# Attention and a gated feed-forward on one core: weight transfers in SyncE's queue, and another grouping in the last tile

## The chip, the core and the metric

The kernel runs on one core of a Trainium2 chip. A core has a matrix engine (TensorE, PE in the profile, with its weight loads apart as PEld), three engines for elementwise work (VectorE or DVE, ScalarE or ACT, GpSimd or POOL) and SyncE (SP), which computes nothing and issues transfers. Each engine works through its own instruction list in order and waits at semaphores for the others. A transfer (DMA) is issued by an instruction of SP, ACT or POOL, and then 16 DMA engines carry it out. The metric is the time of one execution on the device in microseconds (us).

## The reference

One block of a network on `x` of shape (4, 1024, 256): 16 heads of attention with 16 features each, then a feed-forward part with weights of -1, 0 and 1.

```python
def attention(x, Wqkv, Wout):
    q, k, v = split_heads(x @ Wqkv.T)                    # 16 heads of 16
    scores = q @ k.T / 4
    e = exp(clip(scores - max(scores), -50, 50))
    return join_heads(e / (e.sum() + 1e-6) @ v) @ Wout.T

def feed_forward(x):
    h = silu(x @ w1.T * w1_s) * (x @ w2.T * w2_s)        # 256 -> 1024
    h = gelu(h @ h1.T * h1_s)                            # 1024 -> 1024
    h = gelu(h @ h2.T * h2_s)
    return h @ w3.T * w3_s                               # 1024 -> 256

x = x + layernorm(attention(layernorm(x)))
x = x + layernorm(feed_forward(layernorm(x)))
```

## The kernel before

**Stages.** After a prologue of some 40 us, attention runs to about 640 us, and the feed-forward part from there to the end. Attention goes over 4 batches `b`, 4 groups `g` of 4 heads, 2 halves `h` of 512 queries, and 8 blocks of 128 keys; a *unit* is one (b, g, h). For each pair of heads and block of keys, TensorE makes scores (L470, tile `s`), ScalarE their exponentials (L471, tile `e`, in a ring of 8), and TensorE weighs the values with them (L478, tile `acc`). At a unit's end VectorE copies the accumulator out (`o<-acc`, L270).

**The order.** It is written out by hand. The loop at the end of `tile_fast` alternates between making exponentials and weighing, and calls `side.take()` once in a turn of about three tiles of exponentials. `Side` holds chains of `Step`s; a step is taken when the number of turns in its `gap` has passed since the chain's last step, and its flag `tensor` says whether it needs TensorE. What a step issues goes into the lists of its engines at that place. The chains that matter here:

- `stack` (L432): 32 copies of 64 KB (L418) from the projections `cq`/`ck` into the tiles `sq` and `sk`, from which the scores of the next group but one are made. All are issued by SP. There are two sets of these tiles, so that a set has to land before its group begins.
- `divide` (L500): at a unit's end SP stores `top`, the running largest exponentials, to DRAM (`top_d<-top`, L505), and two turns later (`back`, L508) loads them in another layout (`folded<-top_d`). VectorE reduces them (`fold`, L512), TensorE transposes the accumulator (`po`, L517), and VectorE divides. In SP's list both transfers stand between the stack copies.
- `load_rest` (L195): the remaining inputs, by SP, one in a turn: rows of `x` for later batches, `wo_sb`, scales.
- `round_weights` (L243): rounds the weights of the feed-forward part once, in 22 blocks of 512 KB: `load` to the tile `w` (one buffer), `cast` to `wr` (one buffer[...]) on GpSimd, and a store to the DRAM tile `rounded`. Load and store are issued by GpSimd, the store in the step that casts. `load_weights` (L745, SP) reads `rounded` from 567 us on.

GpSimd has few other tasks in this stage: putting values into slots (`vaug`, L448), the powers in the norms (`rstd`, L105), and small squares (`sum`, L350).

**The feed-forward part** goes over 8 tiles of 512 tokens. In each, `gated` makes the first product, `gelu_layer` twice the next two (L802), and `finish` (L842) the last: 4 runs of 128 tokens, each 16 matmuls (L855: 8 blocks of weights, with a high and a low half). In seven tiles the norm and the residual that follow are spread over the next tile by `side`. In the last tile `finish` does them itself, for two runs at a time: product with `w3s_sb` (L857), statistics (L95, L96), `ve` (L103), the power on GpSimd (L105), scaling (L113), residual (L863), and one store a run (L867).

A flag in `bad`, counted along the way, says whether the fast path was valid; the program ends with a branch on it (L67, L68).

Of the kernel before, what the change touches and what calls it, by code (L numbers as in the profile page):

```python
# [9 lines left out]
F32 = mybir.dt.float32  # L10
# [28 lines left out]
TPQ = NQ // P  # L39
# [77 lines left out]
def tile_fast(ctx: ExitStack, tc: tile.TileContext, x, wqk, wv, wo, w1, w1s, w2, w2s, h1, h1s, h2, h2s, w3, w3s, out, bad):  # L117
    nc = tc.nc
# [20 lines left out]
    def pieces(h, view):  # L139

        t, n = NH + (TPQ - 1) * h, TPQ * h
        return (slice(n, n + 1), view[:, h : h + 1, :]), (slice(n + 1, n + TPQ), view[:, t : t + TPQ - 1, :])
# [19 lines left out]
    weights = {"w1": w1, "w2": w2, "w3": w3, "h1": h1, "h2": h2}  # L162
    rows_at_once = {n: WIDE // w.shape[1] for n, w in weights.items()}
# [4 lines left out]
    rounded = {n: dram.tile(list(w.shape), F32R, name=f"{n}_r") for n, w in weights.items()}  # L168
# [11 lines left out]
    with ExitStack() as actx, ExitStack() as rctx:  # L180
# [62 lines left out]
        def round_weights(n, c):  # L243

            st = {}

            def rows(w):
                return w[c * P : (c + rows_at_once[n]) * P, :].rearrange("(i p) d -> p i d", p=P)

            def load():  # L250
                st["w"] = work.tile([P, WIDE], F32, tag="w", name="w", bufs=1)
                nc.gpsimd.dma_start(out=st["w"].rearrange("p (i d) -> p i d", i=rows_at_once[n]), in_=rows(weights[n]))

            def cast():
                st["r"] = work.tile([P, WIDE], F32R, tag="wr", name="wr", bufs=1)
                nc.gpsimd.tensor_copy(st["r"], st["w"])
                nc.gpsimd.dma_start(out=rows(rounded[n]).bitcast(F32), in_=st["r"].bitcast(F32).rearrange("p (i d) -> p i d", i=rows_at_once[n]))

            return [Step(load, 1, False), Step(cast, 3, False)]

        def by_slots(o, w, i, **flags):

# [474 lines left out]
        halves_of = [(b, h) for b in range(B) for h in range(NH)]  # L737
# [18 lines left out]
        def norm_steps(tiles, st):  # L756


            def gather(i):
                def run():  # L760
                    st["mv"] = norms.gather(tiles()[i : i + 2], i, st.get("mv"))

                return run

            def root():
                st["ln"] = norms.root(st["mv"])

            return [Step(gather(i), 1, False) for i in range(0, TPQ, 2)] + [Step(root, 0, False)]
# [73 lines left out]
        def finish(n, i):  # L842

            b, h = halves_of[n]
            st = {}
            z = both.tile([P, TPQ, D], F32, tag="y", name=f"z_{n}", bufs=1)

            pairs = [ps.tile([P, 2, NQ], F32, tag="big", name="pz") for _ in range(TPQ // 2)]
            p = [pairs[t // 2][:, t % 2, :D] for t in range(TPQ)]
            for t0 in range(0, TPQ, 2):  # L850
                ts = range(t0, t0 + 2)
                for c in range(HC):
                    for t in ts:
                        for k, half in enumerate(i):
                            nc.tensor.matmul(p[t], half[:, c, t * P : (t + 1) * P], homes["w3"][c], start=c == 0 and k == 0, stop=c == HC - 1 and k == 1)  # L855
                for t in ts:
                    nc.vector.tensor_mul(z[:, t, :], p[t], w3s_sb)  # L857
                if n == len(halves_of) - 1:

                    ln = norms.stats([z[:, t, :] for t in ts])  # L860
                    for j, t in enumerate(ts):
                        norms.apply(z[:, t, :], z[:, t, :], ln, j)
                        nc.vector.tensor_add(z[:, t, :], z[:, t, :], xs[b][:, h * TPQ + t, :])  # L863
                        for at, tokens in pieces(h, out[b].rearrange("(t p) d -> p t d", p=P)):
                            k = h * TPQ + t - at.start
                            if 0 <= k < at.stop - at.start:
                                nc.sync.dma_start(out=tokens[:, k, :], in_=z[:, t, :])  # L867
            if n == len(halves_of) - 1:
                return []

            def apply(i0):
                def run():
                    for t in range(i0, i0 + 2):
                        norms.apply(z[:, t, :], z[:, t, :], st["ln"], t)

                return run

            def add(t):
                def run():
                    nc.vector.tensor_add(z[:, t : t + 2, :], z[:, t : t + 2, :], xs[b][:, h * TPQ + t : h * TPQ + t + 2, :])  # L880

                return run

            def store():
                for at, tokens in pieces(h, out[b].rearrange("(t p) d -> p t d", p=P)):
                    nc.sync.dma_start(out=tokens, in_=z[:, at.start - h * TPQ : at.stop - h * TPQ, :])

            return (
                norm_steps(lambda: [z[:, t, :] for t in range(TPQ)], st)
                + [Step(apply(i), 1, False) for i in range(0, TPQ, 2)] + [Step(add(t), 1, False) for t in range(0, TPQ, 2)] + [Step(store, 0, False)]  # L890
            )
# [41 lines left out]
        def feed_forward():  # L933

            chain = ends[B - 1, NH - 1]
            checks = check_weights()
            for n in range(len(halves_of)):

                gated(ffn["a"], 2 if n else 1)
                if n + 1 < len(halves_of):  # L940
                    chain[0].extend(prepare(n + 1, to_scalar))

                if 1 < n < len(halves_of) - 1:
                    size = -(-len(checks) // (len(halves_of) - 3))
                    side.add(sum(checks[size * (n - 2) : size * (n - 1)], []) + (judge() if n == len(halves_of) - 2 else []))
                gelu_layer(ffn["b"], ffn["a"], "h1")
                gelu_layer(ffn["a"], ffn["b"], "h2")
                side.flush()
                chain = side.add(finish(n, ffn["a"]), True)
            side.flush()  # L950
# [36 lines left out]
        begin(0)  # L987
        side.add(stack(0, 1) + few(load_rest(), 1))
        side.add([s for k in blocks for s in round_weights(*k)])
        made = seen = weighed = 0  # L990

# [7 lines left out]
        while weighed < len(tiles):  # L999
            n = end = made  # L1000
# [3 lines left out]
            if made == len(tiles):  # L1004
                n = made
# [4 lines left out]
            if n - weighed >= 4 and made - weighed + TURN - 2 <= RING and tiles[weighed][3] != NT - 2 and side.next_is_heavy():  # L1010
                n = weighed + 2
# [257 lines left out]
```

## Time and profile before

| | |
|---|---|
| median of 3 runs | 1302.34 us (1301.2 to 1303.02) |
| profiled execution, its own time | 1304.9 us |
| its span, first to last instruction | 1303.1 us |
| mean granted TensorE clock | 0.990 |
| loads of a block of weights by POOL (L252) | 22: 6 with a median of 6.1 us to landing, 16 with 6.4 |
| stores of a block by POOL (L257) | 22: 4.6 and 4.0 us |
| casts of a block on POOL (L256) | 22 of 1.04 us (median), from 43 to 394 us |
| last instruction of VectorE | ends at 1295.05 us |

How to read the views of the profile: a group of instructions is named by its line and engine and the tiles that it writes and reads (`out<-in`). "Idle before" is the time that the engine stood still just before, with what ended it after an arrow. The chain that ended last is followed back from the last instruction, at each step to what released it. Engines with a q (SPq) are queues of instructions that issue or wait. A window view has one line for a stretch of time: its length, then busy time and number of instructions of PE, PEld, DVE, ACT and POOL, the granted TensorE clock, the busy share of the DMA engines, and GB/s. In the DMA view, a line of an issue ends with the median time from issue to landing; q1 (hardware_dynamic) is the queue of SP, q0 (software_dynamic) that of POOL.

### The profile page before, as it was taken

The numbers are of one execution on the slowest core, as the hardware profiler recorded it, in microseconds if no ns is written. First come the engines' busy times: TensorE is split into PE (matmuls) and PEld (weight loads), VectorE is DVE, ScalarE is ACT, GpSimd is POOL, SyncE is SP. The second block draws the span as 40 slices with busy tenths as digits, with TensorE's granted clock in tenths as the row PEclk, the third lists the DMA queues.
The fourth block names the chain that finished last, engine by engine and source line by source line (L and its number), as shares of the span: only waits on it lengthen the run. The fifth ranks groups of instructions, "written<-read, shape, count | busy, mean of one in ns | idle before, by whom it ended". The sixth has DMA issues, their size and how long they took to land.

```text
span 1303.1 us, 21108 instructions
## 1 busy us (share of the span) xinstructions
PE 1246.2 (96%) x8104; PEld 771.5 (59%) x8104; DVE 700.2 (54%) x1578; ACT 721.6 (55%) x902; POOL 119.4 (9%) x166
## 2 busy tenths in 40 slices
PE   7998899999989999989999999999999999999995
PEld 2333333333333333323688888888888888888885
DVE  3465447763577545656653634636446464463533
ACT  3897898899888998998521413314233142231410
POOL 6221012211111000000000000000000000000000
PEclk8998999999999999999999999999999999999998
DMA  4775745666553544453230000201102011020000
GB/s 131 205 185 137 190 116 144 163 174 153 137 125 77 98 83 98 92 129 120 82 146 1 25 1 1 65 25 34 56 1 66 25 33 57 1 65 9 17 1 20
DMA packets 65678, 107.02 MB, mean 82 GB/s; under 512 B 12960, under 2 KB 39200, under 8 KB 65568
## 3 DMA queue, kind: packets, MB, share of 16 engines
q1 hardware_dynamic: 57680, 80.93, 25.4%
q0 software_dynamic: 7360, 24.12, 6.0%
q8 instruction: 66, 1.08, 0.3%
q10 hardware_dynamic: 528, 0.52, 0.2%
q14 instruction: 44, 0.36, 0.1%
HBM read 48.38 MB, written 23.59 MB: 55 GB/s over the span
## 4 chain that ended last, share of the span: by engine, by line
PE 74%; ACT 10%; DVE 8%; issue 3%; DMA 2%; POOL 1%; SPq 1%; ACTq 0%; POOLq 0%; DVEq 0%
PE ph L802 36%; PE acc L478 12%; ACT e L471 8%; PE s L470 8%; PE pz L855 4%; PE pg L802 4%; PE p L264 4%; PE py L264 2%; PE pv L264 2%; DVE sg L818 2%; PE po L517 1%; DVE ha_lo L807 1%; DVE top L487 1%; DVE st L95 1%; ACT sg L816 1%
## 5 line engine op out<-in xcount | busy, mean ns | idle before, releaser
L471 ACT ACTIVATE e<-s 128x1024 f32<-128x1024 f32 x512 | 483.8, 1043 | 43.6 <-PE s L470 36.2
L478 PE MATMUL acc<-e,vaug 128*32 128x512 f32 x2048 | 257.3, 605 | 1.0 <-POOL vaug L448 1.0
L838 ACT ACTIVATE a<-ph,h_scale 128x512 f32<-128x512 f32 x128 | 81.0, 685 | 301.4 <-PE ph L802 301.4
L470 PE MATMUL s<-sq,sk 64*128 64x512 f32 x1024 | 189.5, 447 | 22.2 <-ACT e L471 17.2
L802 PE MATMUL ph<-hb_hi,h 128*128 128x512 f32 x512 | 199.6, 390 | 0.0
L802 PE MATMUL ph<-hb_lo,h 128*128 128x512 f32 x512 | 199.4, 390 | 0.0
L470 PEld LDWEIGHTS s<-sq,sk 64*128 64x128 f32 x1024 | 87.3, 186 | 144.0 <-ACT e L471 116.5
L487 DVE TENSOR_TENSOR top<-top,e 128x512 f32<-128x512 f32 x192 | 134.0, 698 | 31.7 <-ACT e L471 26.5
L105 POOL TENSOR_TENSOR rstd<-ve,minus_half 128x4 f32<-128x4 f32 (+1 forms) x33 | 37.0, 1122 | 826.2 <-DVE ve L103 826.2
L478 PEld LDWEIGHTS acc<-e,vaug 128*32 128x32 f32 x2048 | 49.4, 109 | 106.5 <-issue 100.2
L802 PEld LDWEIGHTS ph<-hb_hi,h 128*128 128x128 f32 x512 | 96.1, 188 | 20.2
L802 PEld LDWEIGHTS ph<-hb_lo,h 128*128 128x128 f32 x512 | 96.2, 188 | 20.0
L839 DVE CAST ha_hi<-a 128x512 fp32r<-128x512 f32 x64 | 27.1, 423 | 142.7 <-ACT a L838 142.7
L802 PE MATMUL ph<-ha_hi,sq 128*128 128x512 f32 x256 | 101.9, 398 | 0.4
L802 PE MATMUL ph<-ha_lo,sq 128*128 128x512 f32 x256 | 99.9, 390 | 0.0
L802 PE MATMUL ph<-ha_lo,sk 128*128 128x512 f32 x256 | 99.8, 390 | 0.0
L802 PE MATMUL ph<-ha_hi,sk 128*128 128x512 f32 x256 | 99.8, 390 | 0.0
L816 ACT ACTIVATE sg<-pg,w_scale 128x512 f32<-128x512 f32 x64 | 43.3, 688 | 56.0 <-DVE ha_lo L807 45.6
L818 DVE SCALAR_TENSOR_TENSOR sg<-pg,w_scale,sg 128x512 f32<-128x512 f32 x64 | 47.1, 745 | 46.3 <-ACT sg L816 46.1
L839 DVE CAST hb_hi<-a 128x512 fp32r<-128x512 f32 x64 | 27.0, 422 | 71.5 <-ACT a L838 71.5
L264 PE MATMUL p<-xT,wqk_sb 128*32 128x512 f32 x512 | 61.3, 600 | 3.7 <-DVE on L495 1.4
L802 PEld LDWEIGHTS ph<-ha_hi,sq 128*128 128x128 f32 x256 | 48.1, 188 | 13.1 <-DVE sg L818 3.4
(164 smaller groups left out, 1637.3 us busy)
## 6 DMA issues: line engine op xcount, KB each, us to landing
w<-in_h_dram POOLq DMA_DIRECT2D x16, 512.0 KB, 6.4
h_r<-wr POOLq DMA_DIRECT2D x16, 512.0 KB, 4.0
x<-in_h_dram SPq DMA_DIRECT2D x32, 256.0 KB, 2.6
top_d<-top SPq DMA_DIRECT2D x30, 256.0 KB, 2.3
folded<-top_d SPq DMA_DIRECT2D x30, 256.0 KB, 3.2
sk<-ck1hi SPq DMA_DIRECT2D x64, 64.0 KB, 2.7
sk<-ck1lo SPq DMA_DIRECT2D x64, 64.0 KB, 2.7
sq<-cq1hi SPq DMA_DIRECT2D x64, 64.0 KB, 2.5
```

Of the source, the lines that this page charges most:

```text
L105: nc.gpsimd.tensor_tensor(rstd[:, :n], ve[:, :n], self.minus_half[:, :n], ALU.pow)
L264: nc.tensor.matmul(o[j : j + SLOT, :], w[:, j : j + SLOT], i, **flags)
L470: nc.tensor.matmul(s[:, a, :], stacks[1, g % 2, u][r, c * P : (c + 1) * P], stacks[0, g % 2, u][r, h * NQ : (h + 1) * NQ], start=True, sto ...
L471: nc.scalar.activation(pair(k)[:, u], s, AF.Exp)
L478: nc.tensor.matmul(acc[SLOT * i : SLOT * (i + 1), :], vaug[g % 2][:, c, i, :], pair(k)[:, i // 2, i % 2, :], start=c == 0, stop=c == NT - 1)
L487: nc.vector.tensor_max(top, top if c > 1 else pair(k - 2)[:, :, :, 0:P], pair(k)[:, :, :, 0:P])
L802: nc.tensor.matmul(p, homes[n][c][:, m * P : (m + 1) * P], half[:, c, :], start=c == 0 and k == 0, stop=c == len(homes[n]) - 1 and k == 1)
L816: nc.scalar.activation(sg, p[:, 0, :], AF.Silu, scale=scales["w1"][:, m : m + 1])
L818: nc.vector.scalar_tensor_tensor(sg, p[:, 1, :], scales["w2"][:, m : m + 1], sg, ALU.mult, ALU.mult)
L838: nc.scalar.activation(a, p[:, j, :], AF.Gelu, scale=scales[n][:, m : m + 1])
L839: nc.vector.tensor_copy(o[0][:, m, :], a)
L855: nc.tensor.matmul(p[t], half[:, c, t * P : (t + 1) * P], homes["w3"][c], start=c == 0 and k == 0, stop=c == HC - 1 and k == 1)
```

## The change

In `round_weights`, load and store are issued by SP instead of GpSimd. The store is taken out of the step `cast` and becomes a step of its own, two turns later. In `finish`, for the last tile alone, the runs of tokens are grouped as (0, 1), (2), (3) instead of (0, 1), (2, 3): the matmuls of run 2 are all issued ahead of those of run 3, and each of the two has its own statistics, power and scaling.

```diff
             def load():
                 st["w"] = work.tile([P, WIDE], F32, tag="w", name="w", bufs=1)
-                nc.gpsimd.dma_start(out=st["w"].rearrange("p (i d) -> p i d", i=rows_at_once[n]), in_=rows(weights[n]))
+                nc.sync.dma_start(out=st["w"].rearrange("p (i d) -> p i d", i=rows_at_once[n]), in_=rows(weights[n]))
 
             def cast():
                 st["r"] = work.tile([P, WIDE], F32R, tag="wr", name="wr", bufs=1)
                 nc.gpsimd.tensor_copy(st["r"], st["w"])
-                nc.gpsimd.dma_start(out=rows(rounded[n]).bitcast(F32), in_=st["r"].bitcast(F32).rearrange("p (i d) -> p i d", i=rows_at_once[n]))
-
-            return [Step(load, 1, False), Step(cast, 3, False)]
+
+            def store():
+                nc.sync.dma_start(out=rows(rounded[n]).bitcast(F32), in_=st["r"].bitcast(F32).rearrange("p (i d) -> p i d", i=rows_at_once[n]))
+
+            return [Step(load, 1, False), Step(cast, 3, False), Step(store, 2, False)]
...
-            for t0 in range(0, TPQ, 2):
-                ts = range(t0, t0 + 2)
+
+            for ts in [(0, 1), (2,), (3,)] if n == len(halves_of) - 1 else [(0, 1), (2, 3)]:
                 for c in range(HC):
                     for t in ts:
                         for k, half in enumerate(i):
```

The changed kernel is two lines longer from the store on, so that L418, L470 and L855 of before are L420, L472 and L857 of after.

## Prediction

> **What bounds the kernel now.** I read the engines and the whole chain first, then the windows by unit of attention, then the chain in the odd units, then the DMA queues, then the end.
>
> ```profile
> PE 1246.2 (96%) x8104; PEld 771.5 (59%) x8104; DVE 700.2 (54%) x1578; ACT 721.6 (55%) x902; POOL 119.4 (9%) x166
> ...
> PE 74%; ACT 10%; DVE 8%; issue 3%; DMA 2%; POOL 1%; SPq 1%; ACTq 0%; POOLq 0%; DVEq 0%
> ```
>
> TensorE bounds the span; POOL, whose queue is relieved, is 9% busy and 1% of the chain. DMA and SP's queue hold 3% of the chain, some 39 us, and the chain of waits puts all of it before 165 us. So the edited transfers can pay only there. The windows, cut where accumulators are copied out, show it unit by unit (length, then busy time of PE, PEld, DVE, ACT, POOL, granted clock):
>
> ```profile
> 87.50:112.10 24.60, 20.62 (x142) 7.25 (x141) 11.03 (x23) 17.92 (x22) 1.81 (x2) 0.86 0.45 104
> 112.10:129.60 17.50, 16.87 (x133) 6.32 (x137) 11.31 (x20) 16.06 (x20) 5.42 (x8) 1.00 0.84 194
> 129.60:151.90 22.30, 18.92 (x148) 6.62 (x141) 8.83 (x21) 17.21 (x21) 0.93 (x2) 0.92 0.74 189
> ```
>
> The first and third are longer than the second by 7.1 and 4.8 us, and the clock fell in them. The timeline tells the first:
>
> ```profile
> 97.83 0.53 SPq L505 DMA_DIRECT2D top_d<-top  x1
> ...
> 100.46 0.36 SPq L508 DMA_DIRECT2D folded<-top_d  x1
> ...
> 103.24 0.75 DVE L512 TENSOR_TENSOR folded<-folded 128x256 f32<-128x256 f32 x2 [5.37 <-DMA folded<-top_d]
> ...
> 104.82 1.12 PE L517 MATMUL po<-ident,o 128*128 128x128 f32 x4 [3.57 <-DVE cq0lo L330]
> ```
>
> VectorE waits 5.37 us for `folded`, and TensorE 3.57 us behind VectorE. Its unit ended at 87.5, but SP reached the store of `top` at 97.83: from 70.72 on SP issued 37 DMAs without pause. At 0.62 us each, the pace of L418, that is 22.9 us, not 27.1: 4.2 us are lengthened issues and gaps. From 111.35 to 147.3 SP issues 48 DMAs, again late, with 5.7 us of such excess, and at 146.89 TensorE had waited 1.93 us for the last `sq` copy. Both stalls are followed by the half clock: 0.50 in 103.43:110.26 and in 147.81:151.22.
>
> What lengthens SP's issues is the other queue. Shares of the engines in 193:196, just after a store and a load by POOL at 191.3 and 191.8, then landing times of `folded` in 64:165 (POOL's transfers present) and in 402:560 (none):
>
> ```profile
> q0 software_dynamic: 199, 0.75, 93.2%
> q1 hardware_dynamic: 25, 0.04, 3.3%
> ...
> folded<-top_d SPq DMA_DIRECT2D x5, 256.0 KB, 4.4
> ...
> folded<-top_d SPq DMA_DIRECT2D x9, 256.0 KB, 3.2
> ```
>
> SP's queue moves almost nothing while POOL's has data, so `folded` takes 4.4 instead of 3.2 us (8.1 at worst), and `sk<-ck1lo` 4.8 instead of 2.3.
>
> **What the Trainium skill says.** "DMA: Bandwidth & Descriptors", Queues, rings and completion order: each of the 16 engines goes round its queue rows and drains a whole packet before it switches. The 93.2% against 3.3% agree as to direction, and are more one-sided than turn by turn. The same page, Issuing engines are not separate DMA queues: starting DMAs from several engines saves only the time to initiate them; by that the move costs SP 44 issues and little else, and the 3.2 to 4.4 us show that the choice of queue matters here beyond it. "TensorE: Matmul & The Clock Gate", Part 1: a free-running window of some 3.4 us with too little work halves the clock. The trace agrees: TensorE was busy 1.25 us in 100:103.43 and 1.22 in 144.4:147.81, and each was followed by 0.50.
>
> **Part 1, the transfers.** Removed: 44 POOL issues (22 loads, 22 stores) at 0.53 to 0.60 us, some 25 us of POOL; worth nothing, as POOL waits 826 us for `ve` alone. Added: 44 SP issues at 0.62 us (an estimate from the 64 KB copies), 27 us. SP's queue waits 89.5 us, 15 times, for the last `top` of a unit in 33:395; those waits hide the issues outside 70.7 to 98 and 111 to 147. The built program's order leaves TensorE, ScalarE and VectorE as they were up to the last tile. A block's steps take 6 turns instead of 4, so the last store moves from 395 to about 535 us; the first reader (L745) issues at 567.7: 32 us to spare. On POOL only the casts move, later.
>
> New waits: the cast waits for a load in SP's queue, and the store (SP) for the cast. Behind the store stand SP's stack copies and `back`, for which TensorE and VectorE wait. I put each block into the trace's times: load issued after its SP neighbour, landed 4.7 us later, cast 1.2 us, not before its POOL neighbour. Of the 22 casts the tightest ends 4.7 us before SP gets to its store, and none ends after its next POOL instruction is due. So no new stall; price 0, and without that cover up to 5 us each.
>
> In the two stretches where SP is late:
> - 70.72 to 97.83: one store (before the copy at 83.21) and one load (at 87.97) come in: 2 x 0.62 = 1.2. Their own bulk: in the reload of h2 512 KB pass every 1.3 us (landings 656.28, 657.95, 659.21), of which I take half as felt by SP, 0.7 each: 1.4 (bounds 0 and 2.6). The 4.2 of excess falls to the 0 to 1.2 seen in stretches after 402, say 0.6, to which the 1.4 is added. Net -4.2 + 0.6 + 1.4 + 1.2 = -1.0; bounds -2.4 and, if nothing of the excess was POOL's, +3.8. The wait of 2.27 us for `folded` at 82.3 also shrinks, but the end of this stretch is SP's, so I count nothing.
> - 111.35 to 147.3: one store (123.68) and one load (135.11), again 1.2 + 1.4. Of 5.7 excess some 2.5 is the x loads' own (they land after 4.3 to 4.9 us). Net -5.7 + 2.5 + 2.6 = -0.6; bounds -3.1 and +3.8. With landing quicker too (4.5 to 2.3 us for a late copy), I take 1.5 of the 1.93 us off.
> - The clock: 6.83 and 3.41 us at half cost 3.4 and 1.7 us of TensorE's work. With its gap cut to some 0.4 us the second goes, 1.7; the first gap (3.57 less 1.0) stays wide, 0 taken, 3.4 possible.
> - Small VectorE waits for `folded` at 200 and 259 (0.97, 0.37): they go, 0.3 taken.
>
> Sum: -1.0 - 1.5 - 1.7 - 0.3 = **-4.5**.
>
> **Part 2, the last tile.** The 64 matmuls stay; runs 2 and 3 are no longer interleaved. The timeline of the end:
>
> ```profile
> 1290.48 0.75 DVE L857 TENSOR_TENSOR z<-pz,w3s_sb 128x256 f32<-128x256 f32 x2
> ...
> 1292.65 0.69 POOL L105 TENSOR_TENSOR rstd<-ve,minus_half 128x2 f32<-128x2 f32 x1 [3.78 <-DVE ve L103]
> 1293.39 0.41 DVE L113 TENSOR_SCALAR z<-z,mv,rstd 128x256 f32<-128x256 f32 x1 [0.88 <-POOL rstd L105]
> ```
>
> TensorE is done at about 1289.8; VectorE is busy with runs 0 and 1 until 1290.56. So run 2 comes earlier from TensorE (about 1287.9) and nobody can take it: VectorE's order is written out. Its own chain sets the end. Before: 1290.56 to 1295.05, 4.49. Now, for each run: product 0.33, statistics 0.35 + 0.18, `ve` 0.18, POOL's round trip 0.84, scale 0.42, sum 0.43, four steps of 0.02: 2.8; twice 5.6. One more `ve` and one more trip, that were shared. **+1.1** (bounds 0.9 and 1.3). The last store's 1.7 us and the 6 us to the end of the program remain behind it.
>
> **Sum.** -4.5 + 1.1 = -3.4 against the profiled execution's 1304.9 (span 1303.1, 1.8 around it), so 1301.5; it stood 2.6 above the median 1302.34 of runs from 1301.2 to 1303.02, so 1298.9, said as **1299**. About 0.2% (2.6 us) is what a measurement of this kernel can tell from no change; the forecast lies just beyond it.
>
> **Rivals.**
> - *Hidden: no difference.* SP loses the excess but pays it back with the issues, 0 to -1.5; the tail's 1.1 stands; 1301.9 to 1303.4. For it: net -1.0 and -0.6 above are small differences of larger numbers. Against: the landing times of 402:560.
> - *SP's ring fills: slower.* One mechanism: in the two late stretches each 512 KB stands in the same ring ahead of copies, and they land after it. Excess unchanged, 4 x (0.62 + 1.3) = 7.7, less what slack of the copies takes (about 2), plus 1.1: 1305 to 1309; with another half-clock window of 1.7 to 3.4, up to 1312. It decides once what the four cost exceeds the share of the 9.9 us excess that POOL made. Against it: SP's x loads, 1 MB together, already pass there.
> - *Both stalls vanish: much faster.* 3.57 + 3.4 + 1.93 + 1.7 = 10.6, less 1.1: 1292.8. For it: when the gap at 104.82 falls below about 2 us, the clock would stay up too.
> - *The tail does what it seems to be for*, an earlier finish: only if VectorE waited for TensorE at 1290.56; it did not. It cannot be over 0.8, TensorE's lead; 3 in 100, inside the others.
>
> **How the numbers follow.** Forecast (1295 to 1299.7) 0.40 and much faster 0.12: faster 0.52. Hidden, with what small losses and gains balance: 0.31. Slower 0.17. The range 1292.5 to 1308 takes in the much faster case and the ring's lower end, and leaves out about 2 in 10; the forecast's own range is 1295 to 1301.
>
> **What would show it.** Right: no software queue after 34 us; `folded` near 3.2 us in 64:165; the unit that ends near 112 still over 20 us, the next but one near 19; no half clock near 148; 5.6 us from the third product to the last sum. Wrong: SP waiting at the store for POOL, a cast holding `rstd` or `vaug`, copies landing over 4 us after issue between 400 and 535, or TensorE gaps over 1 us where a group begins.

## The result, and the profile after

The changed kernel took 1295.67 us (median of 5 runs, 1295.29 to 1297.94) where the kernel before took 1302.97 (5 runs, 1301.2 to 1303.48). The ratio is 0.995, with a 95% interval of 0.9936 to 0.9965: faster by 0.5%. The profiled execution of after took 1295.67 us (span 1293.9).

The profiled execution of before took 1304.9 us, 1.9 above its median, and so the two spans differ by 9.2 us where the medians differ by 7.3. Cut at the last copy of an accumulator in attention, at the first `pz` of the last tile and at VectorE's last instruction, the 9.2 us lie so (the last column is what the prediction's sum gives):

| stretch | before | after | difference | predicted |
|---|---|---|---|---|
| to the end of attention | 628.82 | 619.91 | -8.9 | -4.5 |
| from there to the last tile's first `pz` | 653.13 | 652.98 | -0.2 | 0 |
| last tile, first `pz` to VectorE's end | 13.09 | 15.39 | +2.3 | +1.1 |
| VectorE's end to the end of the program | 8.01 | 5.60 | -2.4 | 0 |

Three terms of the sum were wrong, by 4.4, 1.2 and 2.4 us, and the second error, in the tail, offsets part of the other two.

**Attention.** The windows of after, by unit as in the prediction (length, busy time of PE, PEld, DVE, ACT and POOL, clock, DMA share, GB/s):

```profile
87.40:107.70 20.30, 18.71 (x142) 6.31 (x141) 10.86 (x23) 18.08 (x22) 1.04 (x1) 1.00 0.59 151
107.70:124.40 16.70, 16.34 (x129) 6.21 (x133) 10.75 (x20) 15.27 (x19) 2.15 (x3) 1.00 0.67 154
124.40:143.20 18.80, 17.62 (x151) 6.38 (x144) 9.41 (x20) 17.66 (x21) 1.05 (x1) 1.00 0.66 157
```

From copy to copy the three units took 24.6, 17.5 and 22.2 us before and take 20.3, 16.7 and 18.8 now, 8.5 less in all, with no half clock in any of them. The other units together are as long as before within 0.4 us. The timeline of the first of them shows why:

```profile
94.89 0.53 SPq L507 DMA_DIRECT2D top_d<-top  x1
...
97.53 0.35 SPq L510 DMA_DIRECT2D folded<-top_d  x1
...
100.32 0.75 DVE L514 TENSOR_TENSOR folded<-folded 128x256 f32<-128x256 f32 x2 [2.54 <-DMA folded<-top_d]
...
101.92 0.66 PE L519 MATMUL po<-ident,o 128*128 128x128 f32 x4 [0.76 <-DVE cq0lo L332]
```

SP reaches the store of `top` at 94.89 instead of 97.83. All that follows comes 2.9 us earlier, and TensorE's gap shrinks from 3.57 to 0.76 us. What made SP late is visible in SP's own timeline. First before, from about 74 us, where two of the pairs of copies take 2.2 to 2.4 us to issue (GpSimd has just issued a store and a load of a block), then after, where the same two pairs take 1.2, as most pairs do in both:

```profile
73.04 0.54 POOL L257 DMA_DIRECT2D w_r<-wr  x1 [0.30 <-POOL wr L256]
73.58 0.60 POOL L252 DMA_DIRECT2D w<-in_w_dram  x1
...
74.22 2.23 SPq L418 DMA_DIRECT2D sk<-ck1hi  x2
...
78.86 2.42 SPq L418 DMA_DIRECT2D sk<-ck1hi  x2
```

```profile
74.12 1.21 SPq L420 DMA_DIRECT2D sk<-ck1hi  x2
...
77.67 1.23 SPq L420 DMA_DIRECT2D sk<-ck1hi  x2
...
80.89 0.37 SPq L259 DMA_DIRECT2D w_r<-wr  x1
...
85.72 0.41 SPq L252 DMA_DIRECT2D w<-in_w_dram  x1
```

The block's own store and load are issued in 0.37 and 0.41 us, less than a 64 KB copy. The DMA view of after in 64:165 (queues with packets, MB and share; then issues, with the median time to landing) has no software queue any more:

```profile
q1 hardware_dynamic: 13088, 16.28, 66.0%
...
folded<-top_d SPq DMA_DIRECT2D x6, 256.0 KB, 2.9
...
sk<-ck1lo SPq DMA_DIRECT2D x16, 64.0 KB, 2.3
```

`folded` landed after 4.4 us here before, `sk<-ck1lo` after 4.8. The second is the safer sign: in kernel 2 below, whose attention is that of before, the two medians are 3.2 and 4.4.

**The last tile.** The timeline of its end in after:

```profile
1281.41 0.42 DVE L859 TENSOR_TENSOR z<-pz,w3s_sb 128x256 f32<-128x256 f32 x1
...
1281.88 0.58 PE L857 MATMUL pz<-ck1hi,ha_hi 128*128 128x256 f32 x1 [3.09 <-DVE z L859]
...
1285.06 0.28 PE L857 MATMUL pz<-ck1lo,ha_lo 128*128 128x256 f32 x1
1285.38 0.42 DVE L859 TENSOR_TENSOR z<-pz,w3s_sb 128x256 f32<-128x256 f32 x1 [1.09 <-PE pz L857]
...
1287.85 0.42 DVE L865 TENSOR_TENSOR z<-z,x 128x256 f32<-128x256 f32 x1
```

TensorE stands still for 3.09 us ahead of the fourth run's products, until VectorE has read the third run's (`z` L859), and VectorE then waits 1.09 us for TensorE. The 16 products take 3.46 us (2.08 in kernel 1): from 1281.41 to 1284.83 the granted clock was half, and a product follows the last after 0.21 us instead of 0.12.

**The end.** GpSimd's closing DRAIN, the group of line L1265 before and L1267 after (shortest, median and longest in ns, then first and last start):

```profile
L1265 POOLq DRAIN  x3: 50/98/6271, 1295.9 to 1302.8; - x3
```

```profile
L1267 POOLq DRAIN  x3: 38/107/2674, 1290.1 to 1293.6; - x3
```

It lasts 6.27 us in before and ends 7.2 us after VectorE's last instruction; it is the last thing that the program waits for. In after it lasts 2.67 us and ends ahead of SP's own closing instructions.

### The profile page after: what moved, and what is told of

It reads as the page before. It is cut to its first block, busy times and chain, and to the rows that moved or that the text cites. A ratio compares the mean times of both kernels' runs of the same rounds, so it can differ in the third digit from the quotient of the medians.

```text
span 1293.9 us, 21111 instructions
## 1 busy us (share of the span) xinstructions
PE 1243.9 (96%) x8104; PEld 771.4 (60%) x8104; DVE 703.0 (54%) x1579; ACT 721.6 (56%) x902; POOL 93.7 (7%) x123
## 4 chain that ended last, share of the span: by engine, by line
PE 76%; ACT 10%; DVE 8%; issue 3%; DMA 2%; SPq 2%; ACTq 0%; POOL 0%; POOLq 0%; DVEq 0%
PE ph L804 36%; PE acc L480 12%; ACT e L473 8%; PE s L472 8%; PE pz L857 5%; PE pg L804 4%; PE p L266 4%; PE py L266 2%; PE pv L266 2%; DVE sg L820 2%; SPq L420 1%; DVE ha_lo L809 1%; PE po L519 1%; DVE st L95 1%; DVE top L489 1%
## 5 line engine op out<-in xcount | busy, mean ns | idle before, releaser
L472 PE MATMUL s<-sq,sk 64*128 64x512 f32 x1024 | 188.5, 444 | 20.4 <-ACT e L473 17.6
L472 PEld LDWEIGHTS s<-sq,sk 64*128 64x128 f32 x1024 | 86.6, 184 | 141.8 <-ACT e L473 114.2
L804 PEld LDWEIGHTS ph<-hb_hi,h 128*128 128x128 f32 x512 | 96.1, 188 | 20.2
L105 POOL TENSOR_TENSOR rstd<-ve,minus_half 128x4 f32<-128x4 f32 (+2 forms) x34 | 37.2, 1095 | 825.0 <-DVE ve L103 825.0
```

What stands on the lines that cost most here:

```text
L105: nc.gpsimd.tensor_tensor(rstd[:, :n], ve[:, :n], self.minus_half[:, :n], ALU.pow)
L472: nc.tensor.matmul(s[:, a, :], stacks[1, g % 2, u][r, c * P : (c + 1) * P], stacks[0, g % 2, u][r, h * NQ : (h + 1) * NQ], start=True, sto ...
L804: nc.tensor.matmul(p, homes[n][c][:, m * P : (m + 1) * P], half[:, c, :], start=c == 0 and k == 0, stop=c == len(homes[n]) - 1 and k == 1)
```

## The experiments

All ratios are to the kernel before as timed beside each: its median was 1302.97 us beside after, 1303.85 beside kernels 1 to 4, 1303.11 beside 5 to 8 and 1304.43 beside 9 and 10. "Profiled" is the time of the execution from which the columns to its right are read. "Attention" is the time of its last accumulator copy, "unit 4" and "unit 6" the two long units of above, "tail" the last tile's first `pz` to VectorE's end, "end" what follows, "drain" GpSimd's closing DRAIN; all in us.

| kernel | median | ratio (95%) | profiled | attention | unit 4 | unit 6 | tail | end | drain |
|---|---|---|---|---|---|---|---|---|---|
| before | 1302.97 | 1 | 1304.90 | 628.8 | 24.6 | 22.2 | 13.09 | 8.01 | 6.27 |
| after | 1295.67 | 0.9950 (0.9936 to 0.9965) | 1295.67 | 619.9 | 20.3 | 18.8 | 15.39 | 5.60 | 2.67 |
| 1 transfers only | 1294.02 | 0.9921 (0.9907 to 0.9935) | 1294.02 | 620.6 | 20.2 | 18.7 | 13.09 | 5.47 | 2.67 |
| 2 tail only | 1307.21 | 1.0025 (1.0014 to 1.0037) | 1305.18 | 625.6 | 24.3 | 19.7 | 15.62 | 8.96 | 6.27 |
| 3 old queue, new pace | 1301.40 | 0.9986 (0.9978 to 0.9994) | 1304.38 | 628.4 | 22.9 | 24.4 | 13.09 | 7.92 | 6.27 |
| 4 SP's queue, old pace | 1297.69 | 0.9958 (0.9945 to 0.9971) | 1295.29 | 621.7 | 21.9 | 18.6 | 13.10 | 5.55 | 2.67 |
| 5 tiles of their own | 1294.41 | 0.9929 (0.9913 to 0.9945) | 1294.35 | 619.7 | 20.7 | 18.1 | 14.21 | 5.52 | 2.67 |
| 6 loads SP, stores POOL | 1298.06 | 0.9953 (0.9936 to 0.9970) | 1299.45 | 625.5 | 22.4 | 21.5 | 13.08 | 6.12 | 4.48 |
| 7 late blocks, SP | 1291.62 | 0.9904 (0.9888 to 0.9920) | 1291.09 | 617.5 | 19.5 | 17.7 | 13.09 | 5.57 | 2.67 |
| 8 late blocks, POOL | 1294.53 | 0.9929 (0.9913 to 0.9945) | 1293.57 | 617.5 | 19.5 | 17.7 | 13.09 | 8.14 | 6.27 |
| 9 late, held back | 1291.12 | 0.9902 (0.9887 to 0.9916) | 1291.12 | 618.4 | 19.5 | 17.7 | 12.46 | 5.48 | 2.67 |
| 10 blocks in halves, POOL | 1312.80 | 1.0067 (1.0053 to 1.0081) | 1313.15 | 633.6 | 25.8 | 25.2 | 13.09 | 11.68 | 9.86 |

The end of attention takes in the start of the program, which varies by 1.5 us from one execution to another (the first unit's copy stands at 53.6 to 55.1 us). Beyond that, before and kernel 2 have the same program in attention, and 3.2 us lie between them, most of it in unit 6. So the 8.9 us of the first table are one draw: the mean of before, 2 and 3 is 627.6, that of after, 1 and 5 is 620.1, and 7.5 us lie between those (8.0 if the time from the first copy to the last is taken). Where a kernel's profiled execution lies far from its median, the ratio, which is over all executions, decides.

**1, 2. Each part alone.** The first has the three steps and SP's queue of the change with the grouping `[(0, 1), (2, 3)]`; the second is before with the new grouping.

> The changed kernel with the last tile grouped as before: SP's queue and the three steps, tail (0, 1), (2, 3). If the two parts are independent: attention ends (last accumulator copied out) near 620 us as in the changed kernel, TensorE's run 3 no longer waits 3.4 us for VectorE, the tail from the first pz matmul to VectorE's last instruction is 13.1 us instead of 15.4, so about 1293.4 us, 2.3 less than the changed kernel. If the half-clock window at the end of the changed kernel's profile was chance and alone made its tail long: no difference from the changed kernel, 1295.7. Time from VectorE's last instruction to the end: 5.6 us if it goes with the number of POOL's transfers, 8.0 if it goes with the tail.

> The kernel before with only the last tile regrouped. Independent parts: attention ends at 628.8 us as before, tail 15.4 us, end 8.0 us after VectorE: about 1305.2 us, 2.3 more than before. Prediction's own step (VectorE's chain alone, no wait of TensorE): 1304.1. If POOL's closing drain (6.3 us before, 2.7 in the changed kernel) depends on the tail and not on POOL's transfers, it is 2.7 here and the time about 1302.9.

The parts are nearly separate. The transfers alone bring all of the gain, in attention and in the drain; the new tail costs 2.3 to 2.5 us wherever it stands. Alone, the tail costs 0.9 us more: with three groups GpSimd's drain begins 1.85 us after VectorE's end instead of 0.90, and with 6.27 us of drain that is on the path. In after the same delay is covered by SP's closing instructions.

**3, 4. Queue or pace.** The store was made a step of its own as well, so a block takes 6 turns instead of 4. Kernel 3 has only that, kernel 4 only the queue.

Kernel 3, from before:

```diff
+            def store():
                 nc.gpsimd.dma_start(out=rows(rounded[n]).bitcast(F32), in_=st["r"].bitcast(F32).rearrange("p (i d) -> p i d", i=rows_at_once[n]))
-            return [Step(load, 1, False), Step(cast, 3, False)]
+            return [Step(load, 1, False), Step(cast, 3, False), Step(store, 2, False)]
```

Kernel 4, from before:

```diff
-                nc.gpsimd.dma_start(out=st["w"].rearrange("p (i d) -> p i d", i=rows_at_once[n]), in_=rows(weights[n]))
+                nc.sync.dma_start(out=st["w"].rearrange("p (i d) -> p i d", i=rows_at_once[n]), in_=rows(weights[n]))
...
-                nc.gpsimd.dma_start(out=rows(rounded[n]).bitcast(F32), in_=st["r"].bitcast(F32).rearrange("p (i d) -> p i d", i=rows_at_once[n]))
+                nc.sync.dma_start(out=rows(rounded[n]).bitcast(F32), in_=st["r"].bitcast(F32).rearrange("p (i d) -> p i d", i=rows_at_once[n]))
```

> Transfers in POOL's queue, but in three steps (6 turns a block, store 2 turns after the cast), tail as before. Theory queue (the software queue holds the DMA engines while it has data, at any pace): the stalls at about 104 and 147 us stay for the most part, attention ends at 626 to 629 us, 1300 to 1303 us. Rival pace (fewer transfers in a time, store and next load no longer back to back): attention ends near 620 us, about 1294 to 1296 us.

> Transfers in SP's queue, but store in the step of the cast (4 turns a block, as before), tail as before. Theory queue: attention ends at 620 to 622 us, 1293.4 to 1296 us, with SP waiting for POOL's cast at some stores. Rival pace: as before, 1301 to 1303 us. Rival of the separate step (SP's waits for the cast hold up its copies): SP waits of several us a store and 1305 us or more.

The profiled execution of kernel 3 is the second longest of 17, that of kernel 4 the shortest of 6, so their 628.4 and 621.7 us of attention overstate the difference. The ratios, over all executions, say that the pace alone gains some 1.8 us (0.9986), the queue alone 5.5 (0.9958), and both together, kernel 1, 10.3 (0.9921). Some 2.5 us of each of the last two are the shorter end, so that attention gains about 2, 3 and 8 us. So the queue is a cause at either pace, with some 6 us at the new one (kernel 3 against 1) and some 3 at the old one. The store's own step is a cause too: it brings 4 to 5 us once the queue is SP's (kernel 4 against 1, whose intervals do not overlap). Kernel 4 shows one way in which it can. First what SP waited for (total us, times, longest), then the gap that is left in unit 4:

```profile
SPq L257 <- POOL wr L256: 22.9, 8, 7.8
```

```profile
103.66 0.66 PE L517 MATMUL po<-ident,o 128*128 128x128 f32 x4 [2.38 <-DVE cq0lo L330]
```

With the store right behind the cast, SP stands still for GpSimd at 8 of the 22 stores, up to 7.8 us; in after it waits 0.3 us at two of them. The gap was followed by no half clock in this execution, whose mean granted clock was 0.995; in the other five it was 0.990 to 0.993. How the 4 to 5 us divide between these waits and the denser traffic was not measured.

**6. Which of the two transfers.** As kernel 1, with the stores left on GpSimd.

```diff
-                nc.sync.dma_start(out=rows(rounded[n]).bitcast(F32), in_=st["r"].bitcast(F32).rearrange("p (i d) -> p i d", i=rows_at_once[n]))
+                nc.gpsimd.dma_start(out=rows(rounded[n]).bitcast(F32), in_=st["r"].bitcast(F32).rearrange("p (i d) -> p i d", i=rows_at_once[n]))
```

> Old tail, blocks' loads from SyncE's queue, stores from GpSimd's, three steps as in the kernel after. Theory, any large transfer in the software queue holds up the copies behind it in time: half of the gain in attention, the fourth unit between 20.3 and 24.6 us (near 22), span of attention 4 to 5 us longer than with both in SyncE's queue. Rival, the loads alone did the harm: attention ends as with both in SyncE's queue (620 us). Rival, the stores alone: as with both in GpSimd's (628 us). For the end: if GpSimd's closing drain goes by the number of its DMAs it lies between 2.7 and 6.3 us (near 4.5, then no longer the last thing: end 5.5 us after VectorE's last instruction); if any DMA in the last part of its queue is enough, it stays at 6.3 us and the end at 8 us.

Windows of its units 4 and 6:

```profile
88.29:110.71 22.42, 19.73 (x142) 6.84 (x141) 10.93 (x24) 17.95 (x22) 1.56 (x2) 0.92 0.52 140
127.66:149.18 21.52, 19.38 (x152) 6.71 (x145) 8.78 (x20) 17.61 (x21) 2.35 (x2) 0.92 0.74 187
```

Both are again lengthened, each with a half clock (0.92). Attention ends at 625.5, which alone decides little, since kernel 2 with both transfers in the software queue ended it at 625.6. The ratio decides: had the stores done all the harm, only the 1.9 us of the shorter end would be gained, a ratio of 0.9985, and it is 0.9953 (0.9936 to 0.9970); had the loads done it all, the time would be near that of kernel 1 (0.9921). So about half of the gain in attention is lost, and both transfers have a part; the reverse, stores in SP's queue alone, was not run. The drain is 4.48 us, the middle, and still gates the end: 6.12 us, not the 5.5 that were expected.

**7, 8. Where the software queue matters.** As kernel 1, but the chain of blocks waits 32 steps at its beginning; all but two loads and one store then lie after 165 us. Kernel 7 has them in SP's queue, kernel 8 in GpSimd's.

```diff
-        side.add([s for k in blocks for s in round_weights(*k)])
+        side.add([Step(lambda: None, 32, False)] + [s for k in blocks for s in round_weights(*k)])
...
-            return [Step(load, 1, False), Step(cast, 3, False), Step(store, 2, False)]
+            return [Step(load, 1, False), Step(cast, 2, False), Step(store, 1, False)]
```

> Old tail, both transfers in SyncE's queue, but the chain of blocks begins 32 steps later (about 165 us instead of 35 us), at a closer pace, so that no block is moved while the first units run. Theory, the blocks' transfers delay the copies that SyncE issues late in the first units: the stall that is left near 100 us (VectorE idle 2.5 us before the folded sums) goes, and attention ends 1 to 3 us earlier than with the blocks early in the same queue (near 618 to 619.5 us). Rival, that stall comes from SyncE's own issues and waits, with no block in it: attention ends at 620.5 us within 0.5, the fourth unit still 20.2 us.

> As the late blocks in SyncE's queue, but both transfers in GpSimd's. Theory, a software transfer costs time only where SyncE is late, in the first 165 us: attention ends within 1 us of the late blocks in SyncE's queue (near 619 us), and only GpSimd's closing drain (6.3 us) makes the kernel 2.4 us longer than that one. Rival, it costs the engines something wherever it lies: attention ends near 628 us, or loses its 8 us spread over the units from 165 us on.

Kernel 8 in the DMA view of 165:560, then in the windows of its units 4 to 6:

```profile
q1 hardware_dynamic: 25132, 33.80, 40.5%
q0 software_dynamic: 5904, 21.50, 16.9%
...
folded<-top_d SPq DMA_DIRECT2D x22, 256.0 KB, 3.2
```

```profile
87.83:107.38 19.55, 18.72 (x142) 6.33 (x141) 10.86 (x24) 18.08 (x22) 0.00 (x0) 1.00 0.38 74
107.38:124.10 16.72, 16.37 (x129) 6.18 (x132) 10.79 (x21) 15.30 (x19) 1.76 (x3) 1.00 0.67 165
124.10:141.76 17.66, 17.23 (x152) 6.28 (x145) 8.70 (x19) 17.22 (x21) 0.00 (x0) 1.00 0.52 119
```

Nearly all of the 22 blocks go through the software queue there, and attention ends at 617.5 us, as it does with SP's queue. A software transfer costs the engines nothing where SP waits for the units, and several us where SP is late. What is left between kernels 7 and 8 is the drain: 8.14 less 5.57 is 2.6 us, and the medians differ by 2.9. Kernel 7 also shows what the blocks cost in SP's own queue: units 4 and 6 are 0.7 and 1.1 us shorter than in kernel 1. It was expected that the wait for `folded` at 99 us would go; it only fell from 2.44 to 1.81, and so that rest is there with no block near.

**10. What the software queue charges by.** Before, with each block transfer cut into two of 64 partitions.

```diff
-                nc.gpsimd.dma_start(out=st["w"].rearrange("p (i d) -> p i d", i=rows_at_once[n]), in_=rows(weights[n]))
+                for q in (slice(0, 64), slice(64, P)):
+                    nc.gpsimd.dma_start(out=st["w"][q].rearrange("p (i d) -> p i d", i=rows_at_once[n]), in_=rows(weights[n])[q])
```

The store is cut in the same way.

> The kernel before, but each of the 44 block transfers in GpSimd's queue is cut into two of 64 partitions each: the same bytes, 88 transfers. GpSimd's closing drain: 2.67 us with none of them, 4.48 us with 22, 6.27 us with 44, a line of 0.082 us each, so 2.67 + 88 x 0.082 = 9.9 us if it goes by the number of transfers, and the end after VectorE's last instruction 8.0 + 3.6 = 11.6 us; if it goes by bytes or packets it stays at 6.3 us. In attention, theory bytes (the block's own packets on the shared DMA engines delay SyncE's copies): attention ends at 628 us within 2 us, as before. Rival, a price per software transfer: it ends at 632 to 637 us.

The DRAIN groups of kernel 6 and of this one:

```profile
L1267 POOLq DRAIN  x3: 44/107/4479, 1292.3 to 1297.4; - x3
```

```profile
L1267 POOLq DRAIN  x3: 50/98/9864, 1300.7 to 1311.1; - x3
```

2.67, 4.48, 6.27 and 9.86 us with 0, 22, 44 and 88 block transfers: 0.082 us for each, with the same 24.12 MB in the queue for 44 and 88. GpSimd issues 32 more DMAs at the start of every one of these kernels, between 16 and 34 us, and 32 x 0.082 is 2.6: the figures fit a drain of 0.082 us for every DMA that GpSimd issued in the whole program. For the block transfers this is shown, however long ago they were (kernel 8 issues the last at 506 us and before at 395, and the drain is the same 6.27); for the 32 it is not, as no kernel is without them. Attention ends at 633.6 us with the same bytes, 4.8 to 8 later than in kernels 2, 3 and before, as was expected of a price per transfer. Packets in the software queue rose too, from 7360 to 8064, so that this run doesn't single out the number of transfers for attention as it does for the drain.

**5, 9. The last tile.** Kernel 5 is after with a product tile for each of the last two runs. Kernel 9 is kernel 7 with the second run's normalising, sum and store moved behind the statistics of the third and fourth.

Kernel 5, from after:

```diff
+            last = n == len(halves_of) - 1
-            pairs = [ps.tile([P, 2, NQ], F32, tag="big", name="pz") for _ in range(TPQ // 2)]
-            p = [pairs[t // 2][:, t % 2, :D] for t in range(TPQ)]
+            pairs = [ps.tile([P, 2, NQ], F32, tag="big", name="pz") for _ in range(TPQ // 2 + last)]
+            p = [pairs[(t + last) // 2 if t > 1 else 0][:, t % 2, :D] for t in range(TPQ)]
```

Kernel 9, from kernel 7:

```diff
-                    for j, t in enumerate(ts):
+                    for ln, j, t in ([(ln, 0, 0)] if ts[0] == 0 else [(first, 1, 1), (ln, 0, 2), (ln, 1, 3)]):
...
+                    first = ln
```

> The kernel after, but in the last tile the third and the fourth run of tokens each have a product tile of their own in PSUM. Theory shared tile: in the kernel after, the last run's 16 products start only when VectorE has read the third run's product, since both lie in one tile, and so TensorE stands still 3.4 us and then works partly at half clock; with tiles of their own the products follow one another without a pause, the last product ends about 3 us earlier, and the tail from the first product to VectorE's last instruction is 13.1 + 1.1 = 14.2 us instead of 15.4: about 1.2 us faster than the kernel after (ratio to before near 0.994). Rival, VectorE's own work on two statistics sets the end: the tail stays at 15.3 to 15.6 us although TensorE ends earlier, and the time is that of the kernel after.

Kernel 5's timeline of TensorE, at the border of the third and fourth run, then of VectorE:

```profile
1278.47 0.28 PE L858 MATMUL pz<-ck1lo,ha_lo 128*128 128x256 f32 x1
1278.59 0.28 PE L858 MATMUL pz<-ck1hi,ha_hi 128*128 128x256 f32 x1
```

```profile
1281.36 0.42 DVE L860 TENSOR_TENSOR z<-pz,w3s_sb 128x256 f32<-128x256 f32 x1
...
1284.16 0.42 DVE L860 TENSOR_TENSOR z<-pz,w3s_sb 128x256 f32<-128x256 f32 x1
...
1286.62 0.42 DVE L866 TENSOR_TENSOR z<-z,x 128x256 f32<-128x256 f32 x1
```

The fourth run's products follow the third's at 0.12 us without a gap, the last is done at 1280.67, and the tail is 14.21: 1.12 longer than with two pairs. The medians of after and this kernel point the same way, but their ratios' intervals overlap; the 1.2 us are read from the traces.

> Late blocks in SyncE's queue and the last tile in two products of two runs, but the normalising, residual sum and store of the second run of tokens are held back until the statistics of the third and fourth have been taken. Theory: VectorE stands still 0.88 us there for GpSimd's root, and 0.41 + 0.43 us less overlap, some 0.8 us, of held work fits into it; the tail from first product to VectorE's last instruction falls from 13.09 to 12.3 us, and the time from 1291.6 to about 1290.9 us, the shortest of all so far. Rival: VectorE is not ready earlier because the last product sets the start of the second pair's statistics; TensorE's last product ends 5.25 us before VectorE's last instruction, VectorE reaches it 4.56 us before, so then only about 0.7 us, or nothing if the product lands later than the profile has it.

Kernel 9's timeline of VectorE:

```profile
1281.12 0.17 DVE L103 TENSOR_SCALAR ve<-mv 128x2 f32<-128x2 f32 x1
1281.20 0.41 DVE L113 TENSOR_SCALAR z<-z,mv,rstd 128x256 f32<-128x256 f32 x1
1281.64 0.43 DVE L865 TENSOR_TENSOR z<-z,x 128x256 f32<-128x256 f32 x1
1282.19 0.41 DVE L113 TENSOR_SCALAR z<-z,mv,rstd 128x256 f32<-128x256 f32 x1
```

The held work stands where VectorE had waited for the power, and the tail is 12.46 instead of 13.09: 0.63 us, by the rival's limit (about 0.7), as the last product sets the start. Such a difference is below what the times tell: kernels 7 and 9 are level, and both beat before and after.

## Why the prediction was right, and where not

The sign was right, and 1295.67 lies in the range and in the forecast's own range; the point was 3.3 us too high, and the change was 7.3 us where 3.4 was said, more than twice as much. That the error isn't larger is in part luck: the tail took back 1.2 us of what attention and the end gained beyond the forecast. By its steps:

- **The cause** was right: the other queue lengthens SP's issues and landings (kernels 1 and 3 differ in nothing but the queue), and it costs time only where SP is late (kernels 7 and 8). The software queue is gone, and the unit next but one takes 18.8 us where near 19 was said. The step of the store's own was rightly given worth, "without that cover up to 5 us each": kernel 4 has waits of up to 7.8. But the reading of `folded`, 4.4 against 3.2, was no safe ground: with the same program in attention kernel 2 has 3.2 in 64:165. One sign of being wrong came true: 10 of 116 stack copies between 400 and 535 us, where the moved blocks now lie, landed after more than 4 us (4.6 at most; none of 112 before). It cost nothing, as no gap of TensorE over 1 us stands there.
- **Stretch 70.72 to 97.83, -1.0.** This term was mis-sized: 27.11 us became 24.26, -2.85. With no block in it the stretch takes 23.51 us in kernel 7, which is the 22.9 of the 37 issues and the 0.6 of rest that the prediction took. Wrong was what the blocks add: 2.6 us, of which 0.75 was measured (24.26 less 23.51). The issues were priced by a 64 KB copy, 0.62, and take 0.37 and 0.41 here; the bulk that SP was to feel, 1.4, is nearly nothing in this stretch.
- **The first half clock, "0 taken, 3.4 possible".** It followed from the last: with 2.85 instead of 1.0 off, the gap is 0.76 and not 2.6, and the half clock is gone. This unit was to be 1.0 shorter and is 4.3 shorter. The half clock was priced too high, though: in the 6.83 us TensorE was busy for 5.44, and its busy time in the unit fell from 20.62 to 18.71, by 1.9 us and not 3.4. The mechanism is that of the rival "both stalls vanish", which had 0.12 and should have had more. Its ground, that below a gap of about 2 us the clock stays up, is not shown: in before the gap of 1.93 us was followed by a half clock.
- **Stretch 111.35 to 147.3, -1.5 and -1.7.** Right: the unit is 3.4 shorter, the gap of 1.93 and the half clock are gone. Of the pieces, what the blocks add was well sized and the excess that goes was put too low: from the store of `top` to the last `sq` copy SP took 33.7 us before, 31.3 in after and 29.1 in kernel 7 with no block, so that 4.6 us of excess went (3.2 said) and the blocks brought 2.2 (2.6 said). The unit between them became 0.8 shorter, which was not counted; what the small waits at 200 and 259 brought lies within the 0.4 by which the other units differ.
- **The ring that fills.** What this rival feared is there: right behind two x loads and the block load at 126.80, copies in SP's queue land after 5.9, 5.6 and 4.9 us in after. It costs little, since SP is no longer late at the end of this stretch: it stands still from 139.85 to 141.79 for the next `top`.
- **The tail, +1.1.** VectorE's chain was right: 14.21 less 13.09 in kernel 5. The step that failed is "the 64 matmuls stay": it looked at how early run 2 comes from TensorE, and not at what run 3 has to wait for. Both runs' products lie in one tile, `pairs[1]`, and in after TensorE doesn't write the fourth run's until VectorE has read the third's; in kernel 5, with a tile for each, it goes on without a wait. The wait of 3.1 us and the half clock around its end cost the other 1.2 us. The sign "5.6 us from the third product to the last sum" failed for the same reason: 6.9 in after, 5.7 in kernel 5.
- **"6 us to the end of the program remain".** They don't: 2.4 us go with the drain, a cost of GpSimd's queue that stands outside attention. The trace of before had it, a DRAIN of 6.27 us, and the prediction put the 44 removed issues at nothing because GpSimd's own time was idle, without looking at what ends the program.

Two statements of the Trainium skill can be set beside the runs. "DMA: Bandwidth & Descriptors", Issuing engines are not separate DMA queues, says that starting DMAs from several engines only saves the time to initiate them. Here the same 44 transfers at the same pace in the other queue (kernels 3 and 1) are worth some 6 us of attention and 2.5 us at the end, so the measurement decides against leaning on it. The same page, Latency and other measured facts, puts the first byte at some 0.6 us from SP's queue and 1 us from GpSimd's; the medians to landing of the 16 blocks of `h1` and `h2` fell by more than those 0.4: loads from 6.4 to 4.6, stores from 4.0 to 3.2 us. No run here shows the first byte itself.

Left open is how a software transfer holds up SP's queue. The runs show where and how much, not whether descriptors, packets or the engines' turns are what SP waits for. The half clock is also not fully understood: the same gap of 2.03 us near 357 to 367 us was followed by one in kernels 3, 6, 8 and 9, and by none in the other eight, before and after among them.

## What to carry to other kernels

Before pricing a moved transfer, find out where its new neighbours in the queue are late: in a stretch where the issuing engine waits anyway, queue and transfer cost nothing, and in one where it is late every lengthened issue can reach TensorE, with a half clock on top. Give a transfer that waits for another engine a step of its own, so that the queue doesn't stand still for it. Where two results share a tile, ask for the reader of the first before making the second a group of its own. Look at the last instruction of the program, too: a drain can gate the end long after the work that filled its queue. And compare the time of a profiled execution with the median before reading a difference of a few us from two profiles.

## What was not expected of the hardware

- GpSimd's closing drain grows by 0.082 us with every block transfer that GpSimd issued, whatever its size and however early: 2.67, 4.48, 6.27 and 9.86 us with 32, 54, 76 and 120 DMAs in all.
- A 512 KB block transfer holds SP no longer than a 64 KB copy: the medians of after are 0.48 us for its loads, 0.41 and 0.52 for its stores, and 0.59 for a stack copy.
- With no block transfer near (kernel 7, 70 to 94 us), SP's pairs of copies are issued in 1.2 us, but for one group of four that took 3.31 us where others took 2.4. Beside software transfers (before, same stretch) pairs take up to 2.4 us. In 64:165 single copies land after up to 7.1 us in before and 5.9 in after.
- A gap of TensorE of about 2 us is followed by a half clock in some executions and not in others: the one near 360 us in 4 of 12 kernels.
